# When two long vector steps and W_in's scale sums are queued in a hand-ordered decoder layer

## Chip, cores and metric

The kernel runs on one core of one Trainium2 chip. The metric is the device time of one launch in microseconds, as the median of several runs. The engines are named as in the profile: PE (TensorE matmul), PEld (its weight loads), DVE (VectorE), ACT (ScalarE), POOL (GpSimd), SP (SyncE, which only issues DMAs).

## What is computed

The input x has 16 sequences of 256 positions with 512 features. Three sublayers follow one another, each on the normalised x and each added back to x:

```python
x = x + mamba2(layernorm(x))                  # the first sublayer
x = x + linear_attention(layernorm(x), ctx)   # sigmoid heads, 16 of them, over a context
x = x + bitlinear_ffn(layernorm(x))           # ternary weights, 8-bit activations

# mamba2, for 32 heads of 64 features and a state of 64:
xz = x @ W_in                                 # gives z, x/B/C and dt
xBC = silu(causal_conv4(xBC) + conv_b)
dt  = softplus(dt_proj + dt_bias);  dA = exp(-exp(A_log) * dt)
h   = dA * h + dt * x * B;  y = h @ C + D * x # a recurrence over 256 positions
out = (rmsnorm(y * silu(z)) * norm_w) @ W_out
```

The change touches two things in mamba2: the softplus that gives the time steps dt, and the scales by which W_in is split into two half-precision parts.

## The kernel before

**Slots and points.** The sequences are taken in 8 pairs. A pair's mamba2 is computed in 16 units, one for each 128 of the 2048 inner features, so there are 128 units and about as many slots. A slot has 8 points. The variable `clock[0]` is the slot times 8 plus the point; below, 56.1 means slot 56, point 1. All of this happens while the program is written: nothing waits for a clock on the chip. The planner only fixes the order in which each engine's instructions are queued, and each engine works its queue off in that order.

**What a slot queues by hand.** For slot s with its unit u0 and the units u1 and u2 before it, the order is:

- Ahead of point 0: DVE multiplies u1's decay matrix with g (`times_g`, L942 and L946, tile `m`), then scans u0's decays (`scan`, L925, tile `m`).
- Ahead of point 1: PE projects the z half of u0 (`project_part`, L687, tile `pp`), and in the middle of it transposes u1's x (`turn_x`, L954, tile `trx`); ACT scales that transposed x (`x_dt`, L964) and takes the silu of z.
- Ahead of point 2: `split_y(u2)`, a cast on ACT (L1000) and a subtraction on POOL (L1001, tile `yl`).
- Ahead of point 3: PE projects the x half of u0.
- Ahead of point 4: PE multiplies u1's matrix with its x (`scan_out`, L974 and L981, tile `py`); ACT starts the convolution (L910) and DVE adds its three taps (`tap`, L704, tile `xs`); ACT squares u2's y and POOL adds the square (L1012, tile `ssq`); ACT takes the silu of the x half (L919); DVE forms y (L989) and gates it (`gated`, L994).
- Ahead of point 5: PE adds u2 to the output product (`out_product`, L1024, tile `po`).

So what is queued on DVE at points 1 and 2 stands between the scan and the taps, and what is queued at points 5 and 6 stands behind the gate and ahead of the next slot's `times_g` and `scan`.

**Side tasks.** Everything else is a Python generator in the list `beside`, sorted by rank (a low number goes first). A task yields a tuple: how many points to wait, at which points it may go on, which engine it will use and for how many microseconds by an estimate in the source. `due` holds a task back when its engine's budget is spent: 2.3 for DVE in a slot (3.6 in the first 18 slots), 2.5 for ACT (4.6 in the first 18). A tuple made by `leaves` carries `True` as its last part, `must`, and is never held back by a budget. `steady()` is true from slot 2 to slot 127.

**Banks.** A side task that multiplies on PE needs room in PSUM. `bank.take` hands out two such places: `own` at point 7, and `z` at point 3. The place `z` is a buffer of the same two that the projections use in turn, so the next projection but one waits until DVE has read it. `crowds()` marks a slot (the next one, when called at points 5 or 6) in which `z` is not handed out.

**Time steps.** `time_steps(pair)` runs once for each pair, in the 16 slots before the pair's own. It multiplies on PE (`pd`), has DVE add the bias (L735 to L742), ACT take an exponential (L744), and then come its two long DVE steps: five instructions of 128x128 (L747 to L751), and nine (L755 to L758). A second exponential (L762), a transpose on PE (L768, tile `pda`), a copy and a small scan on DVE and DMAs follow. Pair 0 is stepped by hand, pair 1 runs in slots 9 to 14, pair 2 in slots 20 to 25, and pairs 3 to 7 begin in slots 37, 54, 70, 86 and 102. For pairs 3 to 7 the first long step is queued at 39.1, 56.1, 72.1, 88.1 and 104.1, and the second one slot later.

**W_in.** W_in lies in 16 chunks of 128 columns for z and x. `scale_units(c0, c1)` squares two chunks on ACT (L455, tile `junk`), sums over partitions with a tiny product on PE (L461, tile `ss_ps`), and turns the sum into scales with five tiny DVE instructions and one for the convolution weights (`scales_from`, L384 to L393, and L466). `prepare(c)` then writes the chunk's two half-precision parts (ACT L481, DVE L483); two may be under way at a time, and chunks 1 to 9 go in order. `keep_w(c)` loads, scales, prepares and stores chunks 10 to 15. The chunks are used in the order 14, 15, 0, 1, 2, 3, 4, 12, 13, 5, 6, 7, 8, 9, 10, 11, one in each slot from slot 0.

After the last slot the feed-forward sublayer runs (L1530 to L1655).

Of the kernel before, what the change touches and what calls it, by code (L numbers as in the profile page):

```python
# [58 lines left out]
def decoder_kernel(  # L59
# [32 lines left out]
    NU = DI // P  # L92
# [9 lines left out]
    NG = 4  # L102
    NP = NB // 2
    NRES = 10
# [90 lines left out]
    with ExitStack() as part:  # L195
# [23 lines left out]
        POINTS = 8  # L219
# [4 lines left out]
        def steady():  # L224
            return 2 * POINTS <= clock[0] < NP * NU * POINTS

        def soon(wait=1):
            return wait if clock[0] >= NP * NU * POINTS else 1

        def dve(us, wait=2):  # L230
            return (wait, (1, 2, 5, 6), "dve", us) if steady() else (soon(2), range(POINTS), "dve", us)

        def act(us, wait=4):
            return (wait, (0, 5, 6), "act", us) if steady() else (soon(3), range(POINTS), "act", us)

# [10 lines left out]
        def landed(wait=8):  # L246

            return (wait if steady() else soon(4)), range(POINTS), None, 0

        def issued():  # L250

            return (4 if steady() else 1), range(POINTS), None, 0
# [5 lines left out]
        def put():  # L258

            return (6 if steady() else 1), range(POINTS), None, 0  # L260

        def leaves(step):

            return *step, True
# [4 lines left out]
        clock = [0]  # L269
# [135 lines left out]
        def load_w(c):  # L405
            if c < NRES - 1:
                raws[c] = place_w(c + 1, (P, 2 * KD * P), F32, "raw")
            else:
                pool_, tag = (q3, "stage") if c < NRES else (q2, "ctx")
                raws[c] = pool_.tile([P, 2 * KD * P], F32, tag=tag, name=f"raw_{c}")  # L410
            nc.sync.dma_start(raws[c], w_zx[c].rearrange("p a k n -> p (a k n)"))
# [11 lines left out]
        def keep_w(c, loaded=False):  # L423

            if not loaded:
                for k in (c, c + 1):
                    load_w(k)
                yield landed(6)
                rank = -3 if c > NRES else -2
                start(clock[0] // POINTS, scale_units(c, c + 2), rank=rank)  # L430
                for k in (c, c + 1):
                    yield from streams.take()
                start(clock[0] // POINTS, prepare(c), rank=rank)
                start(clock[0] // POINTS, prepare(c + 1), rank=rank)
            while not {c, c + 1} <= prepared:
                yield WAIT
            yield issued()
            for k in (c, c + 1):
                nc.sync.dma_start(w16_d[k - NRES], w16[k].rearrange("p h a k n -> p (h a k n)"))
            if c == NRES:  # L440

                return
            yield put()
            for k in (c, c + 1):
                while k not in used:
                    yield WAIT
                streams.give()
# [4 lines left out]
        def scale_units(c0, c1):  # L452
            for c in range(c0, c1):
                yield act(1.3, 1)
                nc.scalar.activation(  # L455
                    junk, raws[c], AF.Square, accum_out=ssq_zx[:, c : c + 1]
                )
            yield (6 if c0 >= NG else 2, (3, 7), "pe", 0.1)
            hold = (yield from bank.take(first=True)) if steady() else "o3"
            pt = misc(hold, [P, c1 - c0], f"ss_ps_{c0}")  # L460
            nc.tensor.matmul(pt, ones, ssq_zx[:, c0:c1], start=True, stop=True)  # L461
            yield dve(1.2, 1)
            scales_from(pt, s_zx[:, c0:c1], inv_zx[:, c0:c1], f"zx{c0}")
            if hold != "o3":
                bank.give(hold)
            nc.vector.tensor_tensor(  # L466
                convw_sb[:, c0:c1, :], convw_sb[:, c0:c1, :],
                inv_zx[:, c0:c1].unsqueeze(2).to_broadcast([P, c1 - c0, 4]), ALU.mult,
            )
            scaled.update(range(c0, c1))  # L470
            yield
# [237 lines left out]
        def time_steps(pair):  # L709

            while ("ready", "m") not in pair:
                yield WAIT
            k = pair["k"]
            hold = yield from bank.take(first=True)
            pd = misc(hold, [P, NT, 2, NH], f"pd_{k}")
            for j in range(2):
                for i in range(NT):
                    n = 0
                    for kc in range(KD):
                        for wi, yi in ((0, 0), (1, 0), (0, 1)):  # L720
                            nc.tensor.matmul(
                                pd[:, i, j, :], pair["lnT"][yi][:, j, i, kc, :],
                                w_dt16[:, wi, kc, :], start=n == 0, stop=n == 3 * KD - 1,
                            )
                            n += 1
            shape = [P, NT * 2, NH]
            v = p1.tile(shape, F32, tag="sp_v", name=f"sp_v_{k}")
            r = p1.tile(shape, F32, tag="sp_r", name=f"sp_r_{k}")
            s = p1.tile(shape, F32, tag="sp_s", name=f"sp_s_{k}")
            s2 = p1.tile(shape, F32, tag="sp_s2", name=f"sp_s2_{k}")  # L730
            q = p1.tile(shape, F32, tag="sp_q", name=f"sp_q_{k}")
            dt = p2.tile(shape, F32, tag="dt", name=f"dt_{k}")
            da = p1.tile(shape, F32, tag="da", name=f"da_{k}")
            yield leaves(dve(0.8))
            nc.vector.scalar_tensor_tensor(  # L735
                v, pd.rearrange("p i b h -> p (i b) h"), inv_dt,
                dtb_sb.unsqueeze(1).to_broadcast(shape), ALU.mult, ALU.add,
            )
            bank.give(hold)
            nc.vector.tensor_scalar(r, v, 0.0, None, ALU.max)  # L740

            nc.vector.scalar_tensor_tensor(v, r, -2.0, v, ALU.mult, ALU.add)  # L742
            yield alone()
            nc.scalar.activation(v, v, AF.Exp)  # L744
            yield dve(1.2)
            crowds()
            nc.vector.tensor_scalar(s, v, 2.0, None, ALU.add)  # L747
            nc.vector.reciprocal(s, s)
            nc.vector.tensor_tensor(s, s, v, ALU.mult)
            nc.vector.tensor_tensor(s2, s, s, ALU.mult)  # L750
            nc.vector.tensor_scalar(q, s2, 1.0 / 15.0, None, ALU.mult)  # L751
            yield dve(1.7)
            crowds()
            for n in (13, 11, 9, 7, 5, 3):
                nc.vector.scalar_tensor_tensor(q, q, 1.0 / n, s2, ALU.add, ALU.mult)  # L755
            nc.vector.scalar_tensor_tensor(q, q, 1.0, s, ALU.add, ALU.mult)
            nc.vector.scalar_tensor_tensor(dt, q, 2.0, r, ALU.mult, ALU.add)
            nc.vector.scalar_tensor_tensor(  # L758
                da, dt, -1.0, ea_sb.unsqueeze(1).to_broadcast(shape), ALU.mult, ALU.mult
            )  # L760
            yield alone()
            nc.scalar.activation(da, da, AF.Exp)  # L762
            pair["dt"] = dt.rearrange("p (i b) h -> p i b h", b=2)
            yield pe(0.1)

            hold = (yield from bank.take(first=True)) if k else "tp"
            pt = misc(hold, [P, P], f"pda_{k}")
            nc.tensor.transpose(pt, da.rearrange("p i h -> p (i h)"), ident)  # L768
            yield leaves(dve(0.4))
            da_t = p1.tile([P, P], F32, tag="da_t", name=f"da_t_{k}")  # L770
            nc.vector.tensor_copy(da_t, pt)
            bank.give(hold)

            ed = p1.tile([P, P], F32, tag="ed", name=f"ed_{k}")
            rows = slice(2 * NH, 4 * NH)
            nc.vector.tensor_tensor_scan(
                ed[rows], da_t[rows], zeros[rows].to_broadcast([2 * NH, P]), 1.0,
                ALU.mult, ALU.add,
            )

            nc.vector.memset(da_t[:, 0:1], 0.0)
            pair["da_t"], pair["ed"] = da_t, ed
            yield issued()
            for i in range(NT):
                nc.sync.dma_start(da_d[k][:, i, :], da_t[2 * NH * i : 2 * NH * (i + 1)])
            nc.sync.dma_start(ed_d[k], ed[rows])
            pair["steps"] = True
            yield
# [938 lines left out]
        def start(slot, gen, every=1, point=0, rank=3):  # L1727
            beside.append(Task(gen, slot * POINTS + point, every, rank))
            beside.sort(key=lambda task: task.rank)
# [389 lines left out]
```

## Time and profile before

| what | value |
|---|---|
| runs | 1876.45, 1879.12, 1882.42 us; median 1879.12 |
| the profiled execution | 1873.6 us, of which the span is 1871.9 us; granted clock 0.992 |
| PE, busy | 1776.4 us, 95% of the span |
| DVE, busy | 1635.6 us, 87% |
| ACT, busy | 1248.1 us, 67% |
| POOL, busy | 684.4 us, 37% |
| slots, first to last | from about 49 us to 1515 us, mostly 10 to 13 us each |

The page's part 5 gives for each group of instructions the busy time, the mean duration, and the idle time just before it with its most frequent releaser. A slot can be found in the trace by counting the L989 instructions on DVE: the n-th of them stands at point 3 of slot n, for n of 2 and more. PE durations are modelled; from one start to the next a 512-wide half-precision matmul takes 0.217 us here, though a single one is listed with 0.38 us.

### The profile page before, as it was taken

To read this page: it belongs to the slowest core of one execution; us is meant where nothing else is said; L and a number is where in the kernel's file an instruction comes from. 1 tells how busy PE (TensorE), PEld (TensorE's weight loads), DVE (VectorE), ACT (ScalarE), POOL (GpSimd) and SP (SyncE) were. 2 spreads that over 40 slices of the span, in tenths; PEclk is the share of its full clock that TensorE was granted. 3 is DMA by queue.
4 is the path that set the end of the run, shared out by engine and by line. 5 is a ranking of instruction groups with operands and counts; after the bars stand their busy time and mean duration, and the time that the engine had idled before them with its cause. 6 is when DMAs were issued, how large, how long until landed. Compare 5 with 4: busy or idle time off the path is not lost.

```text
span 1871.9 us, 30393 instructions
## 1 busy us (share of the span) xinstructions
PE 1776.4 (95%) x10464; PEld 1012.5 (54%) x10464; DVE 1635.6 (87%) x2708; ACT 1248.1 (67%) x2899; POOL 684.4 (37%) x694
## 2 busy tenths in 40 slices
PE   6798899999999999999999999999999999999998
PEld 4454555555556655656555556555656554444443
DVE  6999878778887889898987998989987889999996
ACT  5776566776676665666675666666666657777775
POOL 1232332344334354546453556453533222211000
PEclk9999999999999999999999999999999999999999
DMA  7684776788578777768778779686777825555554
GB/s 220 187 202 142 225 190 172 216 253 260 153 224 251 209 193 256 234 167 234 194 244 215 198 206 279 186 192 170 251 193 204 257 85 113 123 124 126 112 117 96
DMA packets 296933, 358.95 MB, mean 192 GB/s; under 512 B 163765, under 2 KB 197861, under 8 KB 296778
## 3 DMA queue, kind: packets, MB, share of 16 engines
q1 hardware_dynamic: 277962, 296.13, 60.0%
q0 software_dynamic: 18240, 60.84, 9.4%
q8 instruction: 83, 1.36, 0.3%
q14 instruction: 72, 0.59, 0.1%
q10 hardware_dynamic: 576, 0.04, 0.0%
HBM read 279.70 MB, written 39.58 MB: 171 GB/s over the span
## 4 chain that ended last, share of the span: by engine, by line
PE 57%; DVE 26%; ACT 6%; issue 5%; DMA 4%; POOL 3%; SPq 0%; ACTq 0%; POOLq 0%; DVEq 0%
PE pp L687 22%; PE po L1024 12%; DVE xs L704 4%; DVE m L925 4%; PE py L974 4%; PE po_f L1640 4%; PE pg L1598 4%; PE pu L1598 4%; DVE m L942 2%; PE trx L954 2%; PE py L981 2%; DVE h L1603 1%; DVE m L946 1%; DVE am_f L1530 1%; DMA wout<-wout_d 1%
## 5 line engine op out<-in xcount | busy, mean ns | idle before, releaser
L687 PE MATMUL pp<-lnT_h_m,w 128*128 128x512 f16 (+1 forms) x2056 | 656.8, 381 | 10.4 <-DVE xs L704 5.1
L687 PEld LDWEIGHTS <-w 128*128 128x128 f16 x3084 | 294.8, 99 | 349.3 <-issue 33.9
L1001 POOL TENSOR_TENSOR yl<-y,yh 128x512 fp32r<-128x512 f32 x128 | 177.8, 1389 | 693.3 <-ACT yh L1000 600.5
L704 DVE SCALAR_TENSOR_TENSOR xs<-pp,convw_sb,xs 128x510 f32<-128x510 f32 (+2 forms) x384 | 286.2, 745 | 144.6 <-ACT xs L910 134.7
L687 PE MATMUL pp<-lnT_l_m,w 128*128 128x512 f16 (+1 forms) x1028 | 390.8, 380 | 0.0
L1024 PE MATMUL po<-wout,yh 128*128 128x512 f32 x1024 | 336.6, 410 | 6.6 <-DMA wout<-wout_d 6.6
L964 ACT ACTIVATE xdt<-trx,dt 128x64 f32<-128x64 f32 x1024 | 223.4, 328 | 155.0 <-PE trx L954 154.8
L925 DVE TENSOR_TENSOR_SCAN m<-dab,starts 128x512 f32<-128x512 f32 x254 | 303.3, 1234 | 0.0
L1024 PEld LDWEIGHTS po<-wout,yh 128*128 128x128 f32 x1024 | 183.5, 189 | 63.3 <-issue 14.1
L919 ACT ACTIVATE xs<-xs 128x512 f32<-128x512 f32 x128 | 80.9, 632 | 186.3 <-DVE xs L704 186.3
L1024 PE MATMUL po<-wout,yl 128*128 128x512 f32 x512 | 203.8, 398 | 1.5 <-POOL yl L1001 1.4
L1598 PEld LDWEIGHTS <-yT 128*128 128x128 bf16 x1024 | 99.6, 98 | 131.3 <-issue 14.5
L933 ACT ACTIVATE m<-edb,m 128x128 f32<-128x128 f32 x508 | 162.7, 396 | 10.2 <-DVE m L925 9.6
L1012 POOL TENSOR_TENSOR ssq<-ssq,sq 128x512 f32<-128x512 f32 x120 | 157.6, 1313 | 28.6 <-ACT sq L1011 27.7
L910 ACT ACTIVATE xs<-pp,convb_sb,convw_sb 128x512 f32<-128x512 f32 x128 | 100.3, 784 | 101.5 <-PE pp L687 101.5
L974 PE MATMUL py<-m,xdt 128*64 128x256 f32 x1024 | 162.0, 395 | 4.9 <-DVE m L946 3.8
L942 DVE TENSOR_TENSOR m<-m,g 128x1024 f32<-128x1024 f32 x128 | 159.7, 1248 | 0.1
L1598 PE MATMUL pg<-w_ffn,yT 128*128 128x512 bf16 x512 | 131.4, 379 | 8.5 <-ACT h L1602 6.4
L1598 PE MATMUL pu<-w_ffn,yT 128*128 128x512 bf16 x512 | 131.4, 379 | 1.4 <-DVE x L1056 1.4
L1640 PE MATMUL po_f<-w_ffn,hT 128*128 128x512 bf16 x512 | 125.2, 379 | 1.7 <-DMA hT<-hq 1.6
L1602 ACT ACTIVATE h<-pg,sg 128x512 f32<-128x512 f32 x128 | 86.0, 683 | 51.9 <-PE pg L1598 51.7
L1024 PEld LDWEIGHTS po<-wout,yl 128*128 128x128 f32 x512 | 96.6, 189 | 28.7 <-POOL yl L1001 5.8
(279 smaller groups left out, 2791.3 us busy)
## 6 DMA issues: line engine op xcount, KB each, us to landing
dab<-da_d SPq DMA_DIRECT2D x127, 512.0 KB
wout<-wout_d SPq DMA_DIRECT2D x112, 512.0 KB
edb<-ed_d SPq DMA_DIRECT2D x127, 256.0 KB
w<-w_d SPq DMA_DIRECT2D x40, 512.0 KB
raw<-in_w_zx SPq DMA_DIRECT2D x16, 512.0 KB
wout_d<-wout SPq DMA_DIRECT2D x16, 512.0 KB
ctxT<-in_ctx_t POOLq DMA_DIRECT2D x16, 512.0 KB, 8.8
x<-in_x SPq DMA_DIRECT2D x16, 512.0 KB
```

Source lines behind the costliest of these rows:

```text
L687: nc.tensor.matmul(dst, w(wi, kc), yT[yi][:, :, kc, :], start=n == 0, stop=n == 3 * KD - 1)
L704: nc.vector.scalar_tensor_tensor(u[:, :, d:S], raw[:, :, 0 : S - d], w[:, j : j + 1], u[:, :, d:S], ALU.mult, ALU.add,)
L925: nc.vector.tensor_tensor_scan(u["m"][:, 4 * j : 4 * j + 4, :].rearrange("p k t -> p (k t)"), u["da"][j].rearrange("p h i t -> p (h i t)") ...
L933: nc.scalar.activation(u["m"][:, 8 + n, :], u["ed"][:, n // 2, n % 2, :], AF.Copy, scale=u["m"][:, 2 * n, P - 1 : P],)
L942: nc.vector.tensor_tensor(m, m, gi.unsqueeze(2).to_broadcast([P, 2, 2, NT * P]), ALU.mult)
L964: nc.scalar.activation(u["xdt"][:, j, i, h, :], u["tr"][:, j, i, h * HD : (h + 1) * HD], AF.Copy, scale=dt[:, i, j, 2 * c + h : 2 * c + h ...
L974: nc.tensor.matmul(py[h * HD : (h + 1) * HD, j, :].rearrange("p (i t) -> p i t", i=NT), xdt[:, j, 0, h, :], m[:, 2 * (2 * j + h) : 9 + 2 * ...
L1001: nc.gpsimd.tensor_tensor(lo, u["y"], hi, ALU.subtract)
L1012: nc.gpsimd.tensor_tensor(pair["ssq"], pair["ssq"], sq, ALU.add)
L1024: nc.tensor.matmul(pair["po"][n], u["yhl"][yi][:, j, i * P : (i + 1) * P], w[:, wi, :], start=c == 0 and p == 0, stop=c == NU - 1 and p == 2,)
L1598: nc.tensor.matmul(dst, yT[:, kc, :], w_ffn[w + kc][:, cols], start=kc == 0, stop=kc == KD - 1)
L1640: nc.tensor.matmul(u["po"], u["hT", k // (KF // 2)][:, k % (KF // 2), :], w_ffn[2 * KD + k // NF][:, (k % NF) * D : (k % NF + 1) * D], sta ...
```

## The change

Four edits, all to what the side tasks yield:

- The two long steps of `time_steps` yield `leaves(behind(...))` in place of `dve(...)`. From slot 16 on `behind` allows points 5 and 6 alone; before that it is `dve`. `leaves` makes both free of DVE's budget.
- `scale_units` yields its last DVE step through `leaves`, so it is free of the budget as well.
- `scale_units` waits 10 points in place of 6 ahead of its product, where the second square is queued before slot 2 and the chunks are 4 or later.
- `keep_w` waits 14 points in place of 6 for its loads where the chunks are not 10 and 11.

```diff
+        def behind(us):
+
+            return (2, (5, 6), "dve", us) if clock[0] >= NU * POINTS else dve(us)
+
...
-                yield landed(6)
+                yield landed(6 if c == NRES else 14)
...
-            yield (6 if c0 >= NG else 2, (3, 7), "pe", 0.1)
+            yield (2 if c0 < NG else 10 if clock[0] < 2 * POINTS else 6), (3, 7), "pe", 0.1
             hold = (yield from bank.take(first=True)) if steady() else "o3"
             pt = misc(hold, [P, c1 - c0], f"ss_ps_{c0}")
             nc.tensor.matmul(pt, ones, ssq_zx[:, c0:c1], start=True, stop=True)
-            yield dve(1.2, 1)
+            yield leaves(dve(1.2, 1))
...
             nc.scalar.activation(v, v, AF.Exp)
-            yield dve(1.2)
+            yield leaves(behind(1.2))
             crowds()
             nc.vector.tensor_scalar(s, v, 2.0, None, ALU.add)
...
-            yield dve(1.7)
+            yield leaves(behind(1.7))
             crowds()
             for n in (13, 11, 9, 7, 5, 3):
```

## The prediction

> **What bounds the kernel now.** I read the page first: engine shares and the chain that ended last.
>
> ```profile
> PE 1776.4 (95%) x10464; PEld 1012.5 (54%) x10464; DVE 1635.6 (87%) x2708; ACT 1248.1 (67%) x2899; POOL 684.4 (37%) x694
> PE 57%; DVE 26%; ACT 6%; issue 5%; DMA 4%; POOL 3%; SPq 0%; ACTq 0%; POOLq 0%; DVEq 0%
> ```
>
> PE has 95 us of idle time in all, so a microsecond that PE no longer waits reaches the end. The waits of PE (total, times, longest, us) say for whom it waits:
>
> ```profile
> PE trx L954 <- ACT xs L919: 21.0, 14, 3.3
> ...
> PE ss_ps L461 <- ACT junk L455: 5.5, 2, 5.4
> ...
> PE py L974 <- DVE m L946: 3.8, 3, 1.8
> ...
> PE pp L687 <- DVE ss_t_zx L384: 3.1, 1, 3.1
> ```
>
> Third, the timeline of DVE, PE and POOL in slots 56 and 57, where pair 4's long steps stand:
>
> ```profile
> 700.54 1.25 DVE L747 TENSOR_SCALAR sp_s<-sp_v 128x128 f32<-128x128 f32 x1
> ...
> 703.61 2.30 DVE L704 SCALAR_TENSOR_TENSOR xs<-pp,convw_sb,xs 128x510 f32<-128x510 f32 x3
> ...
> 711.19 2.92 DVE L755 SCALAR_TENSOR_TENSOR sp_q<-sp_q,sp_s 128x128 f32<-128x128 f32 x6
> 714.15 1.38 DVE L756 SCALAR_TENSOR_TENSOR sp_q<-sp_q,sp_s 128x128 f32<-128x128 f32 x1
> ...
> 716.10 0.68 DVE L1145 TENSOR_TENSOR xa<-xa,pa 128x512 f32<-128x512 f32 x1
> ```
>
> ```profile
> 706.71 1.09 PE L954 MATMUL trx<-ident,xs 128*128 128x128 f32 x4 [2.97 <-ACT xs L919]
> ...
> 725.29 0.65 PE L974 MATMUL py<-m,xdt 128*64 128x256 f32 x4
> ```
>
> ```profile
> 699.50 2.21 POOL L1012 TENSOR_TENSOR ssq<-ssq,sq 128x512 f32<-128x512 f32 x1
> 711.39 1.27 POOL L1001 TENSOR_TENSOR yl<-y,yh 128x512 fp32r<-128x512 f32 x1 [9.68 <-ACT yh L1000]
> 714.09 1.29 POOL L1012 TENSOR_TENSOR ssq<-ssq,sq 128x512 f32<-128x512 f32 x1 [1.43 <-ACT sq L1011]
> ```
>
> Each long step holds back the taps, the taps hold back the silu, and PE stands at `trx`. The steps also overlap POOL's work: L747 took 1.25 us beside POOL and 0.20 us at 310.56, where POOL was idle. Windows (busy us of PE, PEld, DVE, ACT, POOL; granted clock) show the stretch and what follows the wait:
>
> ```profile
> 690.00:730.00 40.00, 35.92 (x196) 20.34 (x195) 38.15 (x52) 27.43 (x63) 16.24 (x18) 0.96 0.64 163
> ...
> 706.00:710.00 4.00, 3.29 (x11) 1.79 (x12) 3.96 (x5) 4.00 (x12) 0.00 (x0) 0.57 0.62 247
> ```
>
> Last, the start, slots 2 to 4:
>
> ```profile
> 62.72 0.58 PE L461 MATMUL ss_ps<-ssq_zx,ones 128*128 128x2 f32 x2 [5.38 <-ACT junk L455]
> ...
> 86.25 0.38 PE L687 MATMUL pp<-lnT_h_m,w 128*128 128x512 f16 x1 [3.06 <-DVE ss_t_zx L384]
> ```
>
> **Long steps, pairs 3 to 7.** The exponential is queued at 55.5, the wait of 2 ends at 55.7, and the first allowed point is 56.5: half a slot later than 56.1. The second goes from 57.1 to 57.5. Waits of PE to be had, from the same timelines of all five pairs: 2.00 + 0.16 (pair 3, where `q` waits behind `kp`, queued behind step two), 2.97 + 0.29 (4), 1.23 + 0.91 (5), 1.26 (6), 2.96 + 0.87 (7), together 12.65. After each of the three long ones matmuls run slow: in pair 4 the transposes and seven matmuls take 3.43 us (706.71 to 710.14) against 1.95 (692.88 to 694.83), so 1.48; pair 7 gives 1.71, and for pair 3 I estimate 1.5. Sum 17.3 us.
>
> What is late next is `times_g`, and with it `py`. Pair 4 worked through: taps from 700.6, gate done 704.2. POOL was idle from 701.7 to 711.4, so step one takes 2.1 us (as at 310.56 to 312.66) instead of 3.07. The L1145 add (0.68) joins it, since slot 56 now hands out `z`; `times_g` (1.9) ends at 708.9. PE, free of the 2.97 and the 1.48, reaches `py` at 708.1 and waits 0.8. Scan 2.3, two chunk instructions (L1495, 0.75) that find the budget free at 57.1, taps 2.3 and gate 1.4 bring DVE to 715.6; step two, nine at 0.33, takes 2.95 instead of 4.91 (711.19 to 716.10); `times_g` ends at 720.5 and `py` waits 0.4 more. A further 0.3 at the next `trx` makes 1.5 us of new waits where 4.74 were. With today's step lengths they come to some 3.3. Five pairs: 17.3 less 5 times 1.5 is 9.8; less 5 times 3.3 is 0.8; with no new wait 17.3. I take 10, since POOL's idle row is the nearest.
>
> The price of the slow matmuls is the granted clock of 0.57 above, after a wait of 2.97 us. [...]
>
> Pair 2 (22.1 and 23.1 to 22.5 and 23.5) has no wait to lose: `times_g` ended 4.6 and 3.4 us ahead of `py` there (319.82 against 324.46, 331.43 against 334.82): 0, at worst 1. Pairs 0 and 1 keep their places. The second exponential, `pda` (its wait of 0.72 stays), the copy and SP's DMAs of the decays (60.1 after 59.1) come a slot later; pair 4's first load is queued in slot 62, some 20 us on, which hides them; uncovered they would cost a few us a pair. `crowds` closes `z` in slots 57 and 58 instead of 56 and 57, so other side tasks change places by half slots: 0, give or take 3.
>
> **Sums of squares.** `keep_w(12)` loads at clock 8, before `steady()`, where `landed` yields 1 whatever it is given; for chunk 10 it stays 6. This edit does nothing. The product of chunks 4 and 5 leaves 2.3 for 2.7, so its 5.38 us wait goes. But the next PE work needs `times_g` (done 60.0), and the output product needs POOL's `yl`, about 1.4 us after ACT's cast that ends at 63.2, and ACT's order up to there is unchanged: the output product ends near 67.1 instead of 69.8, so 2.7 are won. Chunks 12 and 13 are read at 3.5 instead of 4.1, so the 3.06 goes too, and chunks 10 and 11 at 9.5 instead of 10.1 (waits of 1.12 and 0.79). DVE, though, is idle for only 0.2 to 0.4 us in most of slots 3 to 9, so its work sets the pace and the waits are not won twice. Chunk 4 is then prepared at 4.1 instead of 3.2, and 5 to 9 a slot or two later, the last at 12.1 for slot 13; 11 goes to 13.1, 1.28 us in a slot where DVE had 1.5 idle. I take 4, between 0 and the 10.3 of all those waits.
>
> **Sum.** 1873.6 of the profiled execution less 10 and 4 is 1859.6. That execution was 5.5 below the median of the runs, so I predict 1865.
>
> **Rivals.** *Slower: `py` waits more than `trx` did.* The steps now ignore the budget and meet the L1145 add and chunk work behind the gate. With today's lengths and the 3.2 us between `times_g` (722.1) and `py` (725.3), step one costs 3.07 + 0.68 - 3.2 = 0.6, step two 4.91 + 1.4 - 3.2 = 3.1, with a slow tail of 1.5: 5.2 a pair against 3.5 now. That is +8.5, and with nothing won at the start 1887. It decides where waits at `py` pass 3.5 us a pair. For it: DVE is busy 38.15 of the 40 us. Against: POOL is idle behind the gate.
>
> *Given back.* DVE has the same work in the same stretch, and the wait only changes its name; the start gives 3: 1876.
>
> *More.* All waits go, 17.3 and 10.3: 1851. For it: POOL's idle row; against: `yl` may then meet `times_g`, which took 2.41 instead of 1.22 at 104.10.
>
> **How the numbers follow.** About 0.3%, 5.6 us, is what a measurement can tell from no change: faster is below 1873.5, slower above 1884.8. Forecast case 0.55, given back 0.19, slower 0.17, more 0.09. Faster is the first and the last with a little of the second, 0.66; same 0.17; slower 0.17. The forecast case alone spans 1855 to 1872 by the bounds above; with the given-back case the range goes up to 1880, and 1854 takes in part of the last.
>
> **What would show it.** Right: in slots 55 to 59 and their like the waits of `trx` shrink below 0.5, L747 takes 0.2 us, and `py` waits under 1 us for L946; `ss_ps` no longer waits 5.38. Wrong: `py` waiting 2 us and more, or long steps as long as now. If both are as said and the time is not, the side tasks' new places cost it.

## The result and the profile after

The changed kernel takes 1894.04 us in the median of five runs (1888.11 to 1901.34), the kernel before 1879.12 (1875.31 to 1882.42). The ratio is 1.0080, 95% interval 1.0061 to 1.0099: it is slower, by some 15 us, where 14 fewer were forecast. The profiled execution took 1901.3 us (span 1899.6, granted clock 0.987) and is the slowest of the five, while that of before (1873.6) was faster than any of its five. Of the 27.7 us between the two spans some 13 are therefore the spread of the runs; the places can still be read, the sizes less so.

First the page of the changed kernel: the engines, and the chain that ended last.

```profile
PE 1785.9 (94%) x10464; PEld 1015.8 (53%) x10464; DVE 1634.2 (86%) x2708; ACT 1246.3 (66%) x2899; POOL 698.0 (37%) x694
...
PE 53%; DVE 28%; ACT 7%; DMA 6%; issue 4%; POOL 2%; SPq 1%; ACTq 0%; DVEq 0%; POOLq 0%
```

The instructions are the same in number. PE's idle time, span less busy, went from 95.5 to 113.7 us, and PE's busy time grew by 9.5 at a lower clock (0.992 to 0.987). DVE's and DMA's shares of the chain grew, from 26% to 28% and from 4% to 6%.

Second, the waits of PE in the changed kernel (total, times, longest, us):

```profile
PE trx L958 <- ACT xs L923: 18.7, 11, 3.4
PE pp L691 <- DVE xs L708: 13.6, 9, 3.0
...
PE pk L1248 <- ACT zs L908: 5.7, 1, 5.7
PE py L978 <- DVE m L950: 4.6, 3, 2.8
...
PE q L1099 <- DMA lnT_l_q<-lnl_q: 4.3, 2, 2.4
...
PE kv L1348 <- DMA wv<-in_wv: 3.5, 1, 3.5
```

`trx` waits only 2.3 us less. The price stands in the other rows: `pp` for the taps (5.1 before), and `pk`, `q` and `kv`, products of the side tasks. They are planned in new slots, and what they need comes later than PE does.

Third, the stretch of pair 4's long steps, DVE and then PE (PE's rows cut to the first product of a group):

```profile
698.58 0.32 DVE L751 TENSOR_SCALAR sp_s<-sp_v 128x128 f32<-128x128 f32 x1
698.93 0.95 DVE L752 RECIPROCAL sp_s<-sp_s 128x128 f32<-128x128 f32 x1
...
701.31 1.22 DVE L946 TENSOR_TENSOR m<-m,g 128x1024 f32<-128x1024 f32 x1
...
703.05 3.37 DVE L929 TENSOR_TENSOR_SCAN m<-dab,starts 128x512 f32<-128x512 f32 x2
...
710.51 1.91 DVE L759 SCALAR_TENSOR_TENSOR sp_q<-sp_q,sp_s 128x128 f32<-128x128 f32 x6
```

```profile
710.88 0.60 PE L958 MATMUL trx<-ident,xs 128*128 128x128 f32 x4
...
715.29 0.65 PE L978 MATMUL py<-m,xdt 128*64 128x256 f32 x4
...
723.14 0.63 PE L958 MATMUL trx<-ident,xs 128*128 128x128 f32 x4 [1.07 <-ACT xs L923]
```

Here the change does what it says. Both steps stand between the gate and `times_g`, L751 takes 0.32 us where L747 took 1.25, the six instructions of step two take 1.91 where they took 2.92, and neither the next `trx` (710.88) nor the `py` behind step two (715.29) waits. The windows say the same of 690 to 730: PE is busy 38.22 us (35.92 before), at a granted clock of 1.00 (0.96).

```profile
690.00:730.00 40.00, 38.22 (x225) 21.66 (x223) 36.83 (x57) 28.35 (x71) 17.85 (x20) 1.00 0.69 239
```

Yet pair 4's steps no longer stand in slots 56 and 57: they are a slot earlier, at 55.5 and 56.5, and with them much else. Counted slot by slot, from the starts of DVE's `y` (L993 now, L989 before), the changed kernel stands to the one before like this:

| slots | what is there | gained (-) or lost (+) in it, us | standing after it |
|---|---|---|---|
| to 10 | start, sums of squares | -5.5 | -5.5 |
| 10 to 16 | prepared chunks, pair 1's steps | +3.2 | -2.35 |
| 16 to 23 | pair 2's first step | -0.8 | -3.1 |
| 23 | pair 2's second step | +3.25 | +0.1 |
| 24 to 33 | contexts | -0.6 | -0.5 |
| 33 to 37 | in 33 `pk` waits 5.7 for ACT, which had stood 8.9 at a load | +4.3 | +3.8 |
| 37 to 65 | pairs 3 and 4 and all beside them | -0.2 | +3.6 |
| 65 to 80 | pair 5 and all beside it | +18.6 | +22.2 |
| 80 to the last slot | the rest | +3.9 | +26.1 |

So two thirds of the loss lie in slots 65 to 80, and of those 18.6 us only 0.5 in slots 70 to 76, where pair 5's steps are. One place of it is the tile `wv` (first what POOL waited for ahead of the loads, then who waited for them; the last row gives the shortest, median and longest time from issue to landing):

```profile
L1332 POOL DMA_DIRECT2D wv<-in_wv x8: 712/731/764, 322.6 to 1202.1; - x8
...
  DVE m L950: 3.5, 1
who waited for it (us, times):
...
  PE kv L1348: 3.5, 1
...
DMA to landing us min/median/max: 6.3/7.9/14.0
```

The load of `wv` (POOL, 840.2) had stood 3.5 us behind a wait for DVE's `m`, then took 14.0 us to land where none took over 8.7 before, and the product planned for slot 68 kept PE waiting 3.5 us. In the kernel before no product waited for `wv`.

### The profile page after: what moved, and what is told of

It reads as the page before. It is cut to its first block, busy times and chain, and to the rows that moved or that the text cites. A ratio compares the mean times of both kernels' runs of the same rounds, so it can differ in the third digit from the quotient of the medians.

```text
span 1899.6 us, 30394 instructions
## 1 busy us (share of the span) xinstructions
PE 1785.9 (94%) x10464; PEld 1015.8 (53%) x10464; DVE 1634.2 (86%) x2708; ACT 1246.3 (66%) x2899; POOL 698.0 (37%) x694
## 4 chain that ended last, share of the span: by engine, by line
PE 53%; DVE 28%; ACT 7%; DMA 6%; issue 4%; POOL 2%; SPq 1%; ACTq 0%; DVEq 0%; POOLq 0%
PE pp L691 20%; PE po L1028 11%; DVE m L929 5%; DVE xs L708 4%; PE po_f L1644 4%; PE pg L1602 4%; PE pu L1602 4%; PE py L978 4%; DVE m L946 2%; PE trx L958 2%; ACT xdt L968 2%; PE py L985 2%; DVE m L950 1%; DVE y L998 1%; DVE h L1607 1%
## 5 line engine op out<-in xcount | busy, mean ns | idle before, releaser
L929 DVE TENSOR_TENSOR_SCAN m<-dab,starts 128x512 f32<-128x512 f32 x254 | 315.6, 1283 | 0.0
L1028 PEld LDWEIGHTS po<-wout,yh 128*128 128x128 f32 x1024 | 183.7, 189 | 58.2 <-ACT sq L1015 10.8
```

What stands on the lines that cost most here:

```text
L929: nc.vector.tensor_tensor_scan(u["m"][:, 4 * j : 4 * j + 4, :].rearrange("p k t -> p (k t)"), u["da"][j].rearrange("p h i t -> p (h i t)") ...
L1028: nc.tensor.matmul(pair["po"][n], u["yhl"][yi][:, j, i * P : (i + 1) * P], w[:, wi, :], start=c == 0 and p == 0, stop=c == NU - 1 and p == 2,)
```

## The experiments

**Theories.** *One, displacement:* the new rule changes when the two steps come due and frees them of the budget, so the planner gives other slots to other side tasks; that costs the time, and the steps' own places do not. Comparing what the planner queued at each point, 820 of 1582 entries differ from the kernel before, in slots 2 to 116 (an entry that differs is called displaced below). *Two, places* (the prediction's slower rival): the steps behind the gate make `py` wait. *Three:* the edits to W_in cost it. Each ratio below is to the kernel before on the same chip.

**W_in alone.** As the change, but `time_steps` keeps its two lines:

```diff
-            yield leaves(behind(1.2))
+            yield dve(1.2)
...
-            yield leaves(behind(1.7))
+            yield dve(1.7)
```

> The edits of W_in's sums of squares alone (chunk loads, places of the products, `leaves`); the time steps as in the kernel before. Theory 1 (the shuffle of the other side tasks, which the steps' new rule sets off, costs the time): the start is won as in the changed kernel at slot 16, 2.4 us, so 1876 to 1878, and nothing changes after slot 16. Theory 2 (the steps' new places make py wait): the same, 1876 to 1878. Theory 3 (the W_in edits cost it): 1884 or more. Here 32 of the planned places differ from the kernel before, all in slots 2 to 13.

Measured: 1876.53 us, ratio 0.9984 (0.9969 to 0.9999). Theory three falls; this part of the change gains some 3 us. In its profile the start stands 5.3 us ahead from slot 11 to slot 32, and then loses about as much again in slots 32 to 36, 80, 92 and 93, where its plan is that of the kernel before.

**The steps alone.** The change with W_in as before.

```diff
-                yield landed(6 if c == NRES else 14)
+                yield landed(6)
...
-            yield (2 if c0 < NG else 10 if clock[0] < 2 * POINTS else 6), (3, 7), "pe", 0.1
+            yield (6 if c0 >= NG else 2, (3, 7), "pe", 0.1)
...
-            yield leaves(dve(1.2, 1))
+            yield dve(1.2, 1)
```

> The rule on the two long steps alone (behind the gate, out of turn of the budget, `leaves`); W_in as in the kernel before. Theories 1 and 2: the loss less the start's gain, so 2 to 4 us slower than the changed kernel, 1893 to 1899. Theory 3: 1882 or less. 791 planned places differ from the kernel before, slots 12 to 115; 29 from the changed kernel.

Measured: 1896.44 us, ratio 1.0078 (1.0060 to 1.0097). The whole loss is the steps'.

**Their place without the shuffle: step one.** The kernel before, planner untouched; the five instructions of pairs 2 to 7 are put aside at their planned point and issued at point 5 of the slot.

```diff
+            def first():
+                nc.vector.tensor_scalar(s, v, 2.0, None, ALU.add)
...
+            if k < 2:
+                first()
+            else:
+                hooks.append((clock[0] // POINTS * POINTS + 5, first))
...
         def advance(now):
             clock[0] = now
+            for hook in [one for one in hooks if one[0] <= now]:
+                hooks.remove(hook)
+                hook[1]()
```

> Every planned place as in the kernel before (0 differ), but the five instructions of step one (L747 to L751) of pairs 2 to 7 are issued at the start of point 5, behind the gate, half a slot after their planned point. Theory 1: the place itself is neutral or good: the waits at trx behind step one go (2.97 in pair 4, 2.96 in pair 7), some py waits under 1 us come; 1874 to 1879. Theory 2: py waits 0.6 us and more a pair with slow matmuls behind it: 1882 or more.

Measured: 1882.59 us, ratio 1.0016 (1.0002 to 1.0030). The number is just inside theory two's forecast (1882 or more), but its reason is not there: `py` waits 4.9 us for DVE in all, where it waited 3.8, and the longest new wait of PE is 3.1 us at `trx` in slot 23. With step one alone behind the gate, step two follows it by half a slot and stands where the old stall was, so part of the wait only moves: by the slots of its profile pair 2 loses 4.8 us and pair 6 2, pairs 3, 4 and 7 win about 1 each. This run alone did not decide.

**The shuffle without the place.** The change as it is, its planner told the same, but the instructions are issued half a slot ahead of what it books, at point 1, between scan and taps (step one is shown; step two is moved in the same way).

```diff
+            if k >= 2:
+                hooks.append(((clock[0] // POINTS + 1) * POINTS + 1, first))
             yield leaves(behind(1.2))
             crowds()
-            nc.vector.tensor_scalar(s, v, 2.0, None, ALU.add)
...
+            if k < 2:
+                first()
```

> Every planned place as in the changed kernel (0 differ), but the instructions of the two long steps of pairs 2 to 7 are issued at point 1, between scan and taps, where the kernel before has them. Theory 1: the shuffle is all there and the steps' own places matter little: 1890 to 1902, as the changed kernel. Theory 2: the steps are back where they cost nothing more: 1882 or less.

Measured: 1893.87 us, ratio 1.0072 (1.0048 to 1.0096). With the steps back at the old place the loss is all there. Its waits of PE:

```profile
PE pp L691 <- DVE xs L708: 22.8, 12, 3.9
PE trx L970 <- ACT xs L935: 13.4, 10, 3.4
...
PE py L990 <- DVE m L962: 4.7, 3, 2.8
```

With the steps between scan and taps `py` waits 4.7 us for DVE, as it does in the changed kernel (4.6). Whatever it waits for, it is some 8 us here and some 12 in the changed kernel (5 before). The 4 us between them are waits for ACT, 2.0 in slot 23 and 0.8 in each of the slots 72, 88 and 104, and this run is as slow without them. Theory two falls.

**Both places without the shuffle.** Like step one's, with step two at point 5 as well and the second exponential at point 1 of the next slot.

```diff
+            if k < 2:
+                second()
+            else:
+                hooks.append((clock[0] // POINTS * POINTS + 5, second))
...
+            if k < 2:
+                nc.scalar.activation(da, da, AF.Exp)
+            else:
+                hooks.append(
+                    ((clock[0] // POINTS + 1) * POINTS + 1,
+                     lambda: nc.scalar.activation(da, da, AF.Exp))
+                )
```

> Every planned place as in the kernel before (0 differ), but the instructions of both long steps of pairs 2 to 7 are issued at the start of point 5, behind the gate, and the second exponential at point 1 of the next slot. It has the moves that the prediction priced and no shuffle. By the prediction's term for the pairs (10 of 17.3 us won): 1869 to 1872. By what step one alone showed (pair 2 loses 4.8, pairs 3 to 7 together about 0): 1880 to 1886. If the places alone cost what the changed kernel lost: 1893 or more.

Measured: 1872.77 us, ratio 0.9962 (0.9947 to 0.9977), 7.1 us faster. My expectation from step one was wrong, the prediction's own term was near. The four kernels make a square:

| | steps between scan and taps | steps behind the gate |
|---|---|---|
| plan of before | 1 (with W_in's edits 0.9984) | 0.9962 (with W_in's edits, below, 0.9963) |
| plan of the change, W_in's edits in it | 1.0072 | 1.0080 |

With W_in's edits in all four, the plan costs 0.9% in the first column and 1.2% in the second; the place wins 0.2% under the old plan (0.4% without W_in's edits) and nothing that can be told under the new one. The waits of PE in the kernel with both places:

```profile
PE trx L972 <- ACT xs L937: 11.7, 9, 3.3
PE pp L687 <- DVE xs L704: 9.7, 10, 2.8
...
PE py L992 <- DVE m L964: 4.0, 4, 1.8
```

`trx` falls from 21.0 to 11.7, `py` stays about where it was (4.0 for 3.8), and `pp` rises from 5.1 to 9.7. Pair 4 shows where (PE, the rows that wait or begin a group):

```profile
710.69 0.60 PE L972 MATMUL trx<-ident,xs 128*128 128x128 f32 x4
...
715.68 0.65 PE L992 MATMUL py<-m,xdt 128*64 128x256 f32 x4
...
723.00 0.38 PE L687 MATMUL pp<-lnT_h_m,w 128*128 128x512 f16 x1 [1.65 <-DVE xs L704]
725.26 1.06 PE L972 MATMUL trx<-ident,xs 128*128 128x128 f32 x4
```

By slot 57 pair 4 has won 4.9 us; PE is then so far ahead that it wants the bank of a projection before the taps have read it, waits 1.65, is granted a clock of 0.57 in the four microseconds behind the wait (723 to 727), and keeps 1.55 of the 4.9.

**Part of the rule: the budget.** The steps keep their points and are freed of the budget.

```diff
-            yield dve(1.2)
+            yield leaves(dve(1.2))
...
-            yield dve(1.7)
+            yield leaves(dve(1.7))
```

> Only `leaves` on the two long steps: they keep points 1, 2, 5 and 6 and are no longer held back by the budget. 173 planned places differ from the kernel before, slots 12 to 112. If the loss goes with the number of displaced tasks (16.8 us for 791): 1881 to 1885. If the freed budget is what crowds DVE: 1890 or more. If only the rule on points sets off the costly shuffle: 1877 to 1881.

Measured: 1888.24 us, ratio 1.0053 (1.0035 to 1.0071), for 173 displaced entries. The budget had held step two back till the next slot; freed of it, it is queued at point 5 of step one's own slot (56.5 for 57.1), and feed-forward weights move into the place it left. All fourteen instructions then stand in one slot, and in the waits `py` now does wait for DVE, 10.8 us for 3.8:

```profile
PE trx L958 <- ACT xs L923: 24.2, 15, 3.3
PE py L978 <- DVE m L950: 10.8, 10, 1.8
```

Here theory two is right in the main (`py` waits 7.0 us more, of a loss of some 10): two long steps in one slot are too many. The change does not do that; it spaces them by a slot.

**Pair 2 alone, and all but pair 2.** The condition `if k == 2 else dve(...)`, or `if k > 2`, behind both steps of the change, W_in as before.

> The rule on the two long steps for pair 2 alone. 497 planned places differ from the kernel before, slots 22 to 112. If the loss goes with the number of displaced tasks, and pair 2's own wait at py adds 3.3: 1891 to 1896. If the loss needs the displaced steps of pairs 4 and 5 (slots 54 to 80), 1881 to 1885, the wait at py and little more.

> The rule for pairs 3 to 7, not for pair 2. 607 planned places differ, slots 39 to 116. If the loss goes with the number of displaced tasks: 1890 to 1895. If pair 2's move and what it displaces is most of the loss: 1877 to 1884.

Measured: 1882.64 us, ratio 1.0022 (1.0008 to 1.0037), and 1892.52 us, ratio 1.0069 (1.0042 to 1.0096). Pair 2 alone displaces 497 entries for some 4 us, what slot 23 loses by it (3.1 us) and little more: the loss does not go by number. Without pair 2 most of it is there.

**Both gains together.** The W_in edits added to the kernel with both places.

> The W_in edits and both long steps behind the gate, with the plan of the kernel before (32 planned places differ, slots 2 to 13, those of W_in alone). If the two gains add (2.9 and 7.2 us): 1868 to 1871. If DVE has the same work in the same stretch and one gives back what the other wins: 1872 to 1876.

Measured: 1872.03 us, ratio 0.9963 (0.9948 to 0.9977). The 3 us of W_in do not add up: no better than both places alone. These two are the fastest kernels here, both ahead of the kernel before and of the change.

**Shuffles with nothing else in them.** The kernel before with one budget changed, no step given a new rule:

```diff
-        room = {"dve": 2.3, "act": 2.5, "pe": 2.0, "pool": 2.5, "dma": 4.0}
+        room = {"dve": 2.4, "act": 2.5, "pe": 2.0, "pool": 2.5, "dma": 4.0}
```

and in the same way POOL 2.7 for 2.5, and DVE 2.2 for 2.3.

> The kernel before with DVE's budget in a slot 2.4 for 2.3; 416 planned places differ, slots 60 to 112. If any shuffle costs by its size (about 8 us for 400 places): 1885 to 1890. If DVE's crowded slots cost: the same or more, with more waits at pp for the taps than the 5.1 us of the kernel before. If neither: 1877 to 1882.

> The kernel before with POOL's budget in a slot 2.7 for 2.5; 170 planned places differ, slots 55 to 112, as many as by `leaves` alone (173, which cost 8.7 us). If any shuffle costs by its size: 1882 to 1889. If DVE's freed budget made that loss: 1877 to 1882.

> The kernel before with DVE's budget in a slot 2.2 for 2.3; 188 planned places differ, slots 61 to 127. If more room for DVE's side work in a slot is what costs (2.4 cost 18.4 us), less of it costs nothing or gains: 1872 to 1880. If any shuffle costs by its size (170 places cost 5.3 us, 173 cost 8.7): 1882 to 1889.

Measured: 1897.94 us, ratio 1.0098 (1.0077 to 1.0118) for DVE 2.4; 1883.78 us, ratio 1.0028 (1.0010 to 1.0045) for POOL 2.7; 1881.03 us, ratio 1.0027 (1.0010 to 1.0043) for DVE 2.2, whose median lies between the two forecasts. Every one is slower, less room as well as more, and a tenth of a microsecond in DVE's budget costs about as much as the change. But POOL 2.7 and DVE 2.2 cost little. By the number of entries POOL 2.7 fits its forecast, while DVE 2.4 lost some 18 us where its number forecast 8. A fourth kernel, with ACT's budget 2.4 for 2.5, would have displaced 804 entries with nothing else in it, nearly as many as the change; the order that it plans deadlocks, so a pure shuffle of the change's size has no time here. What sets DVE 2.4 apart is that the chains of pairs 5 and 6 (norm, steps, states) begin a slot earlier, at 69.4 and 85.4, as in the change.

**The early chains.** So the last two runs take the change and hold back one task, the norm of pair 4, by 4 or by 12 points:

```diff
-                start(s, norm_pair(pair), rank=-4)
+                start(s, norm_pair(pair), point=4 if pair["k"] in (4,) else 0, rank=-4)
```

By 4 points the chains of pairs 5 to 7 fall back to where they were before; by 12 it is pair 4's that does, and those of 5 to 7 stay early.

> The change, with the start of one side task held back: the norm of pair 4 begins half a slot (4 points) later. The chains of pairs 5, 6 and 7 then begin at 70.375, 86.375 and 102.375 as in the kernel before (a slot earlier in the change); 721 planned places still differ from the kernel before. If the loss comes from the chains that run a slot early and what they push aside in slots 62 to 80: 1874 to 1884. If any displacement of this size costs, wherever it lies: 1889 or more.

> The same task held back by 12 points. Pair 4's chain then begins at 54.375 as before, but those of pairs 5, 6 and 7 a slot early as in the change; 773 planned places differ. If the early chains of pairs 5 to 7 cost: 1888 to 1900, as the change. If holding back the norm, or pair 4's own place, is what helps: 1884 or less.

Measured: 1879.62 us, ratio 1.0010 (0.9997 to 1.0024), and 1894.55 us, ratio 1.0095 (1.0069 to 1.0121). That tells them apart: with 721 and 773 displaced entries, 15 us lie between the two medians. The plan that is early in pairs 5 to 7 costs; pair 4's own chain is early in the cheap one of the two, so it is not what costs. Of the gap between their two profiled executions 9 us lie in slots 62 to 116 and 9 in the first 16 slots, where the two plans are the same and only the runs differ; against the change itself the norm held by 4 points saves 16 us in slots 62 to 116. All kernels in one table (chain: where pair 5's first step on PE is queued; stretch: slots 62 to 116 of the profile, one execution each):

| kernel | displaced | chain | stretch, us | ratio |
|---|---|---|---|---|
| both places | 0 | 70.4 | 623.3 | 0.9962 |
| both gains together | 32 | 70.4 | 622.0 | 0.9963 |
| W_in alone | 32 | 70.4 | 625.1 | 0.9984 |
| before | - | 70.4 | 622.9 | 1 |
| the change, norm held 4 points | 721 | 70.4 | 628.2 | 1.0010 |
| step one's place | 0 | 70.4 | 625.7 | 1.0016 |
| pair 2 alone | 497 | 70.4 | 625.2 | 1.0022 |
| DVE 2.2 | 188 | 70.4 | 626.3 | 1.0027 |
| POOL 2.7 | 170 | 70.4 | 626.6 | 1.0028 |
| budget alone | 173 | 70.4 | 631.1 | 1.0053 |
| pairs 3 to 7 | 607 | 69.4 | 633.9 | 1.0069 |
| the change's plan, old place | 820 | 69.4 | 644.8 | 1.0072 |
| steps alone | 791 | 69.4 | 636.2 | 1.0078 |
| the change | 820 | 69.4 | 644.2 | 1.0080 |
| the change, norm held 12 points | 773 | 69.4 | 637.3 | 1.0095 |
| DVE 2.4 | 416 | 69.4 | 645.9 | 1.0098 |

All six kernels with the early chain take 633.9 us or more in the stretch and are at 1.0069 or more; the ten others take 631.1 or less and are at 1.0053 or less. What goes wrong when the chain is early can be looked for in the windows (columns as before: PE, PEld, DVE, ACT, POOL, granted clock, DMA share, GB/s). Slots 72 to 80 of the kernel before, of the change, and of the two with the norm held by 4 and by 12 points:

```profile
891.61:979.35 87.74, 82.66 (x529) 48.95 (x529) 80.56 (x125) 62.21 (x158) 46.70 (x47) 1.00 0.77 220
```

```profile
906.36:1001.56 95.20, 86.86 (x504) 52.15 (x505) 79.45 (x120) 62.90 (x159) 49.34 (x45) 0.95 0.89 225
```

```profile
890.28:988.54 98.26, 88.96 (x549) 52.63 (x547) 83.78 (x130) 62.51 (x158) 50.61 (x48) 0.98 0.75 207
```

```profile
908.87:1004.05 95.18, 87.02 (x504) 52.16 (x505) 79.47 (x121) 63.01 (x159) 48.67 (x45) 0.95 0.87 225
```

With the chain early the DMA engines are busy for 0.87 and 0.89 of the time in place of 0.77 and 0.75, and PE needs 95 us for fewer instructions, at a clock of 0.95. These rows alone do not settle it: the third stretch is the longest of the four, with more of PE's work in it (549 records for 504) and 9.3 us in which PE does nothing. In DVE 2.4 the crowded slots are 62 to 72 instead (share 0.82 for 0.76).

Loads that land late reach PE in two ways. `kv` waits for `wv` (3.5 us) and `q` for `lnT_l_q` (2.4 us in slot 77) themselves. And ACT stands at feed-forward weights that a side task has queued on it, and what is queued behind them comes late; slot 33 in the table of slots and slot 23 (under pair 2, below) are two such places, where PE then waits for ACT. ACT's waits at the scaling of these weights, in the changed kernel and with the norm held by 4 points:

```profile
ACT wchunk L1497 <- DMA wchunk<-in_w_down_t: 8.8, 3, 4.7
ACT wchunk L1497 <- DMA wchunk<-in_w_up_t: 4.7, 1, 4.7
```

```profile
ACT wchunk L1497 <- DMA wchunk<-in_w_up_t: 2.4, 1, 2.4
ACT wchunk L1497 <- DMA wchunk<-in_w_gate_t: 0.4, 1, 0.4
ACT wchunk L1497 <- DMA wchunk<-in_w_down_t: 0.4, 1, 0.4
```

Added up, such waits come to 9.3 to 18.2 us in the six kernels with the early chain, and to 0.7 to 6.5 in the ten others (5.4 in the kernel before). That plans with the early chains cost is shown. That it is the chains themselves and not other entries that move with them, and that they do it by crowding transfers, is read from these rows and was not tried by itself.

## Why the prediction was wrong

- **The term that failed** is the prediction's "so other side tasks change places by half slots: 0, give or take 3". More than half of all entries moved, long chains by a whole slot, and between the change (1.0080) and the two gains under the old plan (0.9963) that is 1.17%, 22 us. The sentence looked at `crowds` alone, and took each chain to start where it did: "half a slot later than 56.1". It left out that a step moved in one pair gives other tasks its turn and its budget, so that later ones start from other points, and that the chains of pairs 4 to 7 came a whole slot earlier for it. By the stretches of the profiles 9 to 16 of the 22 us go with the early chains of pairs 5 to 7. The forecast of 1865 less this term's zero, plus 22, would have been 1887; the 7 us that are left to 1894 are the two gains, forecast at 14 and measured together at 7.
- **The long steps of pairs 3 to 7**, forecast at 10 us, gave 7.1 in the kernel with both places, by its ratio and by the slots of its profile (4.0, 1.6, 1.1, -0.2 and 0.6 us won for pairs 3 to 7, counted from `y` to `y` of slots 37 to 43, 52 to 62, 70 to 77, 86 to 93 and 102 to 109). The mechanism held: step one takes 2.1 us as said, POOL's row being idle there, the waits of `trx` behind the steps go, and for pair 4 the 4.74 us of wait and slow matmuls that were to be had came out as 4.9. Mis-sized was what is late next: 1.5 us a pair, put at `py` and the next `trx`. `py` behind the steps waits for nothing in pair 4, and the new wait is a slot later, at `pp` for the taps, 1.65 us with a stretch at a granted clock of 0.57 behind it, 2.79 in pair 7. Pair 4 gave back 3.4.
- **In the changed kernel itself** the five pairs' stretches win only some 2.7 us, counted by the same slots, where other tasks stand beside them.
- **Pair 2 at 0, at worst 1:** 0.7 us lost with the old plan, as bounded. In slot 23 of the change it lost 3.25, with `py` waiting 2.0 us for ACT's scaled x at 334.13 where the prediction saw 3.4 us of slack. Ahead of the scaled x ACT had stood at a load of feed-forward weights:

```profile
330.81 0.63 ACT L1462 ACTIVATE wchunk<-wchunk 128x512 f32<-128x512 f32 x1 [4.27 <-DMA wchunk<-in_w_gate_t]
```

- **The start, forecast 4:** by slot 9 it was 5.0; the wait of `ss_ps` is gone, and that of `pp` fell from 3.06 to 0.21. By slot 16 the change has given back 3.2 of it in the slots where the moved chunks meet pair 1's freed steps; W_in alone keeps 5.3 there. What reached the end of W_in alone is 3 us, and beside the steps' gain nothing that can be told. That the edit of `landed` does nothing held in the plan: taken back by itself in W_in alone, it displaces no entry.
- **The slower rival** had the sign and the wrong mechanism: `py` at 3.5 us a pair and more. It waits 4.6 us for DVE there, 2.8 of them in slot 1, and behind the steps of pairs 5 to 7 some 0.8 us each for ACT.
- **What would show it** named the case that came: the steps as said, the time not, and so the side tasks' new places.

The prediction set a granted clock of 0.57, after a wait of 2.97 us, beside the slow matmuls. The runs add a row: with both places, PE waited 1.65 us ahead of 723.0, and the window behind it is granted 0.57 with PE busy throughout:

```profile
723.00:727.00 4.00, 4.00 (x13) 2.00 (x14) 3.85 (x8) 3.20 (x7) 1.36 (x3) 0.57 0.70 264
```

So here a wait of little more than half that length is followed by a slow stretch as well.

## What to carry to other kernels

Where a planner packs the rest of the work by estimates, an edit to one task's conditions is two edits: the move, and a new plan for everything that is queued after it. Print both plans and compare them before believing a sum; look there for long chains that start in another slot, which told more here than the number of entries. If the move is wanted, issue it by hand under the old plan (0.9962 where the rule gave 1.0080), or hold the chain back where it was (1.0010). And when a wait is taken from the path, look for the next one a stage further on, at the buffer that the faster engine will want, not only at the instruction that was moved.

## What the runs showed that was not expected

- DMA engines that were busier moved hardly more: in slots 62 to 80 as a whole the change shows a share of 0.84 at 201 GB/s, the kernel before 0.76 at 211.
- DVE's scan (two instructions) takes 3.37 us beside POOL's work, as at 703.05 of the changed kernel, and 2.33 us at 726.77 of the kernel with both places, where POOL was idle: 1.0 us for one overlap. In slots 62 to 116 DVE is busy 550.9 us (815 records) with both places and 555.9 us (814) in the kernel before.
- PE's busy time grew from 1776.4 to 1785.9 us from before to the change with the same instructions, at a granted clock that fell from 0.992 to 0.987: 9.5 us, beside 18.2 of idle time.
